# Product's groups: the bias added by GpSimd, the norm's factors held in PSUM

## The chip, the cores and the metric

The kernel runs on one core of a Trainium2 chip. The metric is device time in microseconds (us), from the launch's start to its end; lower is better. A profile is one execution of the program, with the start and end of every instruction on each engine: PE is TensorE (PEld its weight loads), DVE is VectorE, ACT is ScalarE, POOL is GpSimd, SP is SyncE, which here only issues DMAs.

## The reference

The input x is one image of 512 x 512 positions with 64 channels, in float32. Two layers are added to it in turn. The first is, cut to what matters:

```python
x = x + L0(gn(x))                       # gn: a group norm over the image

def L0(x):
    xn = ln(x, norm_w, norm_b)          # layer norm over the 64 channels
    left, right = xn @ left_w + left_b, xn @ right_w + right_b
    left, right = left * mask, right * mask         # mask[i, j] = m[i] * m[j]
    left = left * sigmoid(xn @ lgate_w + lgate_b)
    right = right * sigmoid(xn @ rgate_w + rgate_b)
    out_gate = sigmoid(xn @ ogate_w + ogate_b)
    out = einsum('bkjd,bkid->bijd', left, right)    # the triangle product
    out = ln(out, onorm_w, onorm_b) @ out_w + out_b
    return out * out_gate
```

The second layer adds a spectral convolution (the lowest 12 x 12 modes) of gn(x), computed here by small matrix products. The mask m is drawn from 0 and 1, so about half of the rows and columns of the product are zero, and there the layer norm's output is the bias alone.

## The kernel before, in words

The kernel gathers the rows with a mask that isn't zero into K = 256 slots (function compact). After two earlier stages, the triangle product of the 256 slots lies in SBUF as one tile, places, of 128 partitions x 32768 floats; a slot column has two rows of 64 channels per partition.

The stage that the change touches is one loop, from line 1075, over steps s. It is software-pipelined by hand: LEAD = 13 steps lie between the transpose of a piece (step s + 13) and its scaling (step s). The order of the instructions on each engine is the order of the code (tc.manual_schedule); no scheduler moves them. SIZE = 8 steps make a group k. The first 8 groups (first = K * 2 // 64 = 8, so 64 steps) are the **product's groups**: they take the layer norm of the triangle product, multiply it by out_w, add the bias out, and write the result u to a DRAM buffer, u_d. The 32 groups after them (256 steps) are the **x groups**: they do the layer norm and the gate of the input, multiply the gate with u (or with the bias row where the slot is masked), add it to x, take statistics and store.

A step of the product's groups, in the order of the code:

- transpose(s + 13), L927: four PE transposes into t_ps (L933), and a ScalarE copy to xt_y (L936).
- centered(s + 12), L946: sixteen PE instructions into y_ps (L954), which give for each half the centred values and the product with out_w side by side. From step 51 on, the transposes, and from step 52 on the centring, are those of x: L938 and L943 take the place of L936 and L954.
- root(k + 1) at n = 5 of the group's eight steps, L980: ScalarE takes the square root of the variances in totals and writes rss (L982).
- squared(s + 12), L962: ScalarE squares the centred half into sq_c (L971) and copies the other half to xt_c (L972). Tile xt_c has LEAD + 2 = 15 buffers.
- load(k, r), L984: gathers of x by GpSimd for the x groups, an indirect DMA of 1 MB each (L628), two for each group, three groups ahead, at n = 3 and n = 6. The first six are issued in the code at steps 43, 46, 51, 54, 59 and 62.
- summed(s + 11) at every second step, L974: VectorE reduces 128 x 1024 squares to sixteen sums in totals (L976).
- at n = 7 VectorE takes the reciprocal of rss (L1138): these are the norm's factors of the next group.
- VectorE scales the raw product with the factors, broadcast over 64 channels, into a half of z_t (L1144, 128 x 512). At every second step it adds the bias to the whole of z_t (L1147, 128 x 1024), and SP sends it to u_d (L1150, 512 KB). Tile z_t has four buffers.

At step 64, load_u(0) (L990) issues on SP the first 32 of the reads of u_d that the x groups need; each reads one slot.

In the x groups GpSimd does two operations a pair of steps, gated (L1002, a multiply) and added (L1006), both 128 x 1024.

PSUM tile scratch (L913) is one bank, [128, 4, 128] floats. Its first two rows' left halves hold totals, by the group's parity; row 2 holds the two biases, broadcast over the partitions (bias_ps), and row 3 sums for the statistics. The right halves of the first two rows are not used. The bias rows lie in SBUF as well (rows_of). GpSimd reads and writes SBUF only in this kernel.

Of the kernel before, what the change touches and what calls it, by code (L numbers as in the profile page):

```python
# [17 lines left out]
P = 128  # L18
N = 512
C = 64  # L20
# [26 lines left out]
def conv_preact_kernel(ctx: ExitStack, tc: tile.TileContext, t: dict):  # L47
    nc = tc.nc
    x, out = t["x"], t["out"]
# [562 lines left out]
    def compact(fc):  # L612
# [31 lines left out]
        with tc.tile_pool(name="xc", bufs=1) as cp:  # L644
# [48 lines left out]
            with tc.tile_pool(name="fb", bufs=QB + 8) as gp, tc.tile_pool(name="fw", bufs=2) as wk, tc.tile_pool(  # L693
# [7 lines left out]
                gts, totals, rss, rbs, xns, todo = {}, {}, {}, {}, {}, []  # L701
# [86 lines left out]
        rows_of = {}  # L788
# [17 lines left out]
        with tc.tile_pool(name="tri", bufs=1) as trp:  # L806
# [50 lines left out]
            SIZE = 8  # L857
            LEAD = 13
            RING = 5
            first = K * 2 // 64  # L860
# [3 lines left out]
            with tc.manual_schedule(), tc.tile_pool(name="late", bufs=1) as lp:  # L864
# [30 lines left out]
                with tc.tile_pool(name="np_x", bufs=LEAD + 2) as tp, tc.tile_pool(  # L895
# [17 lines left out]
                    scratch = ps_n.tile([P, 4, P], F32, name="scratch")  # L913
                    sum_ps = [scratch[:, 3, i * G : (i + 1) * G] for i in range(2)]
                    bias_ps = {"out": scratch[:, 2, :C], "ogate": scratch[:, 2, C:]}
                    for name, ps in bias_ps.items():
                        nc.vector.tensor_copy(ps, rows_of[name])
                    totals = [scratch[:, i, : SIZE * 8] for i in range(2)]
                    eps = lp.tile([P, 1], F32, name="eps")
                    nc.vector.memset(eps, EPS)  # L920
                    xts, rss, sqs, us, zs, fs, st = {}, {}, {}, {}, {}, {}, {}
# [153 lines left out]
                    for s in range(-LEAD, total_g + 2 * SIZE):  # L1075
                        k, n = divmod(s, SIZE)
# [20 lines left out]
                        if n % 2 == 0:  # L1097
                            i, c = (0, n // 2 - 1) if n >= 2 else (1, 3)
# [11 lines left out]
                        if n % 2 == 1:  # L1110
                            i, c = (0, (n - 3) // 2) if n >= 3 else (1, 3)
# [4 lines left out]
                        else:  # L1116
                            i, c = (0, (n - 4) // 2) if n >= 4 else (1, 2 + n // 2)
# [17 lines left out]
                        if 0 <= s + LEAD - 2 < total_g and (s + LEAD - 2) % 2 == 1:  # L1135
                            summed(s + LEAD - 2)
                        if n == 7 and k + 1 in rss:
                            nc.vector.reciprocal(rss[k + 1], rss[k + 1])  # L1138
                        if wps is not None:
                            c, odd = divmod(n, 2)  # L1140
                            if not odd:
                                z = zp.tile([P, 16, C], F32, name="z_t")
                            rs = rss[k][:, 8 * n : 8 * n + 8].unsqueeze(2).to_broadcast([P, 8, C])
                            nc.vector.tensor_mul(z[:, 8 * odd : 8 * odd + 8, :], wps, rs)  # L1144
                            if odd:
                                bias = bias_ps["out" if k < first else "ogate"]
                                nc.vector.tensor_add(z, z, bias.unsqueeze(1).to_broadcast([P, 16, C]))  # L1147
                                if k < first:
                                    j = JC * k + 8 * c
                                    nc.sync.dma_start(  # L1150
                                        u_d[:, j : j + 8].rearrange("p j r c -> p (j r c)"), z.rearrange("p n c -> p (n c)")
                                    )
                                else:
                                    zs[v, c] = z
# [151 lines left out]
    with tc.If(rows_with_mask < K + 1) as few:  # L1306
        with tc.tile_pool(name="fconst", bufs=1) as fc:
            compact(fc)
# [65 lines left out]
```

## Time and profile before

| what | us |
|---|---|
| median of three runs (lowest, highest) | 1879.58 (1876.83, 1881.99) |
| the profiled execution's own time | 1877.87 |
| span of its instructions | 1876.0 |
| first scaling of a product's group | 690.5 |
| first scaling of an x group | 815.5 |
| last of GpSimd's adds in the x groups begins | 1532.5 |

Over the whole span the engines are busy as follows:

| engine | busy us | share |
|---|---|---|
| PE | 1653.0 | 88% |
| PEld | 1302.6 | 69% |
| DVE | 1454.2 | 78% |
| ACT | 953.8 | 51% |
| POOL | 873.8 | 47% |

How to read it: the page cuts the span into 40 slices of 46.9 us, and gives each engine a digit a slice, its busy share in tenths. A line of a group gives the source line, engine, operation, what it writes and reads, the shapes and the count, then the busy time in us with the mean of one instruction in ns, then the idle time of the engine just before such instructions and what ended most of it. A line of waits reads "who <- for whom: us in total, how often, the longest". The bounds of a stretch (A:B) are us from the span's start, and the first number behind it is its length.

After the x groups, from about 1535 us on, a last stage reads x back, adds the second layer and writes the output; there DMA is busy at nine tenths or more and the other engines mostly wait.

### The profile page before, as it was taken

Reading aid. Unit: us, or ns where it says so; the run is one execution under the profiler, and the core shown is the slowest. Engines: PE = TensorE matmul, PEld = TensorE weight load, DVE = VectorE, ACT = ScalarE, POOL = GpSimd, SP = SyncE. Lnnn points to the kernel's source line nnn. Section 1 sums busy time; section 2 is a strip of 40 time slices with the busy share of each in tenths; the row PEclk is TensorE's granted clock in tenths of the full one; section 3 lists DMA queues with packets and bytes.
Section 4 is the critical chain, followed back from the end, with each engine's and each line's share of the span. In section 5 each row is a group of like instructions: output and inputs, shape, how many; then the busy total and the mean of one; then the engine's idle time right before and its main releaser. Section 6 shows DMA issues by size and latency. Waiting matters only on the chain. (4 is left out here: it accounts for less than half of the span.)

```text
span 1876.0 us, 33850 instructions
## 1 busy us (share of the span) xinstructions
PE 1653.0 (88%) x11598; PEld 1302.6 (69%) x11598; DVE 1454.2 (78%) x3001; ACT 953.8 (51%) x1670; POOL 873.8 (47%) x678
## 2 busy tenths in 40 slices
PE   6779899999899999899998999899989957997873
PEld 5666666664787777788887988788879835664441
DVE  5989677777455559989998899899989994664552
ACT  3665466554222278777776677677757720111000
POOL 3655111111000000059999799989979982111110
PEclk9989899999899999999999999999989976555555
DMA  6999155556655534347876677767666599999999
GB/s 251 390 380 377 59 135 139 140 138 160 206 180 175 168 127 180 136 151 263 267 258 231 226 252 252 266 222 241 235 240 229 189 252 365 414 426 427 426 427 382
DMA packets 188869, 468.23 MB, mean 250 GB/s; under 512 B 35184, under 2 KB 134384, under 8 KB 147600
## 3 DMA queue, kind: packets, MB, share of 16 engines
q1 hardware_dynamic: 158192, 262.40, 41.3%
q0 software_dynamic: 27856, 202.19, 28.0%
q8 instruction: 94, 1.54, 0.3%
q10 hardware_dynamic: 2640, 1.38, 0.3%
q14 instruction: 87, 0.71, 0.1%
HBM read 278.13 MB, written 187.76 MB: 248 GB/s over the span
## 5 line engine op out<-in xcount | busy, mean ns | idle before, releaser
L943 PE MATMUL w_ps<-gate_x,xt_c 128*128 128x128 f32 x2048 | 283.3, 283 | 30.2 <-DVE z_t L1144 28.8
L1006 POOL TENSOR_TENSOR places<-places,z_t 128x1024 f32<-128x1024 f32 x127 | 301.8, 2377 | 8.2
L943 PEld LDWEIGHTS w_ps<-gate_x,xt_c 128*128 128x128 f32 x2048 | 254.4, 195 | 47.5 <-DVE z_t L1144 45.7
L943 PE MATMUL c_ps<-center_x,xt_c 128*128 128x128 f32 x2048 | 277.7, 279 | 6.1 <-ACT xt_c L938 5.5
L943 PEld LDWEIGHTS c_ps<-center_x,xt_c 128*128 128x128 f32 x2048 | 253.5, 195 | 9.9 <-ACT xt_c L938 7.8
L1286 PE MATMUL l_ps<-places,rinv 24*128 24x512 f32 x512 | 211.3, 1128 | 33.2 <-DVE places L1293 27.1
L1051 DVE BATCH_NORM_STATS2 stats2c<-places 128x6 f32<-128x128 f32 x1024 | 220.4, 278 | 8.2 <-POOL places L1006 8.2
L976 DVE TENSOR_REDUCE scratch<-sq_c 128x16 f32<-128x1024 f32 x160 | 194.6, 1216 | 21.7 <-ACT sq_c L971 7.6
L1100 ACT ACTIVATE z_t<-z_t 128x1024 f32<-128x1024 f32 x128 | 135.4, 1058 | 141.9 <-DVE z_t L1147 120.2
L1147 DVE TENSOR_TENSOR z_t<-z_t,scratch 128x1024 f32<-128x1024 f32 x160 | 195.4, 1221 | 11.3 <-ACT rs_n L982 3.3
L1286 PEld LDWEIGHTS l_ps<-places,rinv 24*128 24x128 f32 x512 | 120.9, 304 | 118.5 <-DVE places L1293 74.8
L933 PE MATMUL t_ps<-c_ident,places 128*128 128x128 f32 x1280 | 201.4, 281 | 1.3 <-DVE places L853 1.3
L1002 POOL TENSOR_TENSOR z_t<-z_t,bias_row_out 128x1024 f32<-128x1024 f32 x63 | 149.7, 2376 | 101.2 <-ACT z_t L1100 101.0
L1293 DVE TENSOR_TENSOR places<-places,l_ps 128x512 f32<-128x512 f32 x200 | 124.0, 682 | 89.8 <-DMA places<-x_h,dst_i 58.3
L938 ACT ACTIVATE xt_c<-t_ps,ab_xc 128x512 f32<-128x512 f32 x256 | 176.1, 688 | 34.4 <-PE t_ps L933 27.7
L933 PEld LDWEIGHTS t_ps<-c_ident,places 128*128 128x128 f32 x1280 | 146.6, 143 | 59.6 <-issue 50.4
L628 POOL DMA_INDIRECT places<-in_x,src_i x64 | 62.6, 978 | 258.0 <-PE t_ps L933 247.3
L1144 DVE TENSOR_TENSOR z_t<-w_ps,rs_n 128x512 f32<-128x512 f32 x256 | 171.9, 672 | 7.4 <-PE w_ps L943 7.4
L1002 POOL TENSOR_TENSOR z_t<-z_t,places 128x1024 f32<-128x1024 f32 x64 | 151.5, 2367 | 35.9 <-ACT z_t L1100 35.7
L968 ACT ACTIVATE sq_c<-c_ps 128x512 f32<-128x512 f32 x256 | 150.7, 589 | 31.4 <-PE c_ps L943 31.1
L678 DVE BATCH_NORM_STATS2 stats1c<-x_ps 128x6 f32<-128x512 f32 x256 | 155.3, 680 | 13.4 <-PE x_ps L677 13.4
L663 ACT COPY xc<-xg 128x128 f32 x352 | 105.0, 298 | 67.5 <-POOL xc L663 43.5
(206 smaller groups left out, 2607.5 us busy)
## 6 DMA issues: line engine op xcount, KB each, us to landing
x_h<-places SPq DMA_DIRECT2D x64, 1024.0 KB
out_x<-places SPq DMA_DIRECT2D x50, 1024.0 KB
places<-u_d SPq DMA_DIRECT2D x512, 64.0 KB
left_d<-o_c SPq DMA_DIRECT2D x64, 256.0 KB
right_d<-o_c SPq DMA_DIRECT2D x64, 256.0 KB
left_raw<-left_d SPq DMA_DIRECT2D x64, 256.0 KB
right_raw<-right_d SPq DMA_DIRECT2D x64, 256.0 KB
u_d<-z_t SPq DMA_DIRECT2D x32, 512.0 KB
```

The costliest lines, as they stand in the source:

```text
L678: nc.vector.bn_stats(stats[:, 0, 16 * (jc % quarter) + 4 * r + c, :], ps.rearrange("p i k -> p (i k)"))
L933: nc.tensor.transpose(tps[:, i, :], flat[:, o : o + P], ident)
L938: nc.scalar.activation(xts[s], tps, AF.Identity, bias=ab1[:, 2:3])
L943: nc.tensor.matmul(ps[:, 2 * i : 2 * i + 2, :], xts[s][:, i, :], w, start=True, stop=True)
L968: nc.scalar.activation(sq, cps, AF.Square)
L976: nc.vector.tensor_reduce(totals[k % 2][:, 8 * (n - 1) : 8 * (n + 1)], sqs.pop(s // 2), AX.X, ALU.add)
L1002: nc.gpsimd.tensor_mul(zs[k, c], zs[k, c], u)
L1006: nc.gpsimd.tensor_add(xr, xr, zs.pop((k, c)))
L1051: nc.vector.bn_stats(st[k // 4][:, g, k % 4, :], x_of(k)[:, :, 2 * g : 2 * g + 2])
L1144: nc.vector.tensor_mul(z[:, 8 * odd : 8 * odd + 8, :], wps, rs)
L1147: nc.vector.tensor_add(z, z, bias.unsqueeze(1).to_broadcast([P, 16, C]))
L1286: nc.tensor.matmul(ps.rearrange("p j o -> p (j o)"), rinv[h, b, :], it[h], start=True, stop=True, tile_position=(32 * g, 0),)
```

## The change

It concerns the product's groups alone. Two lists of PSUM columns, factors, take the unused right halves of the first two rows of scratch. The reciprocal of a product group writes there instead of over rss in SBUF, by the group's parity, and the scaling reads its factors from there; its other operand, xt_c, and its output, z_t, stay in SBUF. The bias is added to z_t by GpSimd from the SBUF bias row, where VectorE added it from PSUM. The x groups keep factors in SBUF and the bias on VectorE. Number and size of all instructions stay the same.

```diff
                     totals = [scratch[:, i, : SIZE * 8] for i in range(2)]
+
+                    factors = [scratch[:, i, SIZE * 8 :] for i in range(2)]
...
                         if n == 7 and k + 1 in rss:
-                            nc.vector.reciprocal(rss[k + 1], rss[k + 1])
+                            nc.vector.reciprocal(factors[(k + 1) % 2] if k + 1 < first else rss[k + 1], rss[k + 1])
                         if wps is not None:
                             c, odd = divmod(n, 2)
                             if not odd:
                                 z = zp.tile([P, 16, C], F32, name="z_t")
-                            rs = rss[k][:, 8 * n : 8 * n + 8].unsqueeze(2).to_broadcast([P, 8, C])
+                            rs = (factors[k % 2] if k < first else rss[k])[:, 8 * n : 8 * n + 8]
+                            rs = rs.unsqueeze(2).to_broadcast([P, 8, C])
                             nc.vector.tensor_mul(z[:, 8 * odd : 8 * odd + 8, :], wps, rs)
                             if odd:
-                                bias = bias_ps["out" if k < first else "ogate"]
-                                nc.vector.tensor_add(z, z, bias.unsqueeze(1).to_broadcast([P, 16, C]))
+                                if k < first:
+                                    bias = rows_of["out"].unsqueeze(1).to_broadcast([P, 16, C])
+                                    nc.gpsimd.tensor_add(z, z, bias)
+                                else:
+                                    nc.vector.tensor_add(z, z, bias_ps["ogate"].unsqueeze(1).to_broadcast([P, 16, C]))
```

## The prediction

> **What bounds the kernel now.** I read the page first (its engine shares, slices and costliest groups), then the stretch of the product's groups alone. In the slices GpSimd's row shows zeros over seven of the forty slices while VectorE's climbs to 9:
>
> ```profile
> DVE  5989677777455559989998899899989994664552
> POOL 3655111111000000059999799989979982111110
> ```
>
> The end of the empty run is the product stage. The timeline puts its first scaling at 690.51 us and the first scaling of an x group (step 64) at 815.52: 64 steps in 125.0 us. Busy time over its two parts (before and after the first x transpose comes in, columns PE, PEld, DVE, ACT, POOL, each with its count) says who is full:
>
> ```profile
> 690.50:784.40 93.90, 86.97 (x1000) 71.64 (x998) 89.83 (x104) 78.57 (x156) 2.81 (x3) 0.96 0.42 166
> 784.40:815.50 31.10, 24.60 (x210) 22.41 (x208) 29.86 (x35) 19.70 (x37) 0.00 (x0) 1.00 0.33 136
> ```
>
> VectorE is busy 119.7 of 125.0 us (96%), GpSimd 2.8. PE's 87 of 93.9 looks nearly as full, but its ends are modelled, so I ask the waits of the same two parts who waited for whom:
>
> ```profile
> ACT rs_n L982 <- DVE scratch L976: 8.6, 5, 2.2
> PEld y_ps L954 <- ACT xt_y L936: 8.5, 7, 2.3
> PE y_ps L954 <- ACT xt_y L936: 6.9, 5, 2.1
> ...
> PEld c_ps L943 <- ACT xt_c L938: 6.9, 6, 1.5
> ACT xt_c L938 <- DVE z_t L1144: 5.8, 4, 1.7
> ```
>
> In the first part ScalarE's root stands still for VectorE's reduce once a group, and PE then stands still for ScalarE. In the second, ScalarE waits for a buffer of xt_c that VectorE's scaling frees. VectorE is the bound of both. Its groups in the stretch:
>
> ```profile
> L1144 DVE TENSOR_TENSOR z_t<-xt_c,rs_n 128x512 f32<-128x512 f32 x64 | 41.2, 675 | 0.0
> L976 DVE TENSOR_REDUCE scratch<-sq_c 128x16 f32<-128x1024 f32 x33 | 40.5, 1228 | 4.9 <-ACT sq_c L971 1.3 <-ACT xt_y L936 0.5
> L1147 DVE TENSOR_TENSOR z_t<-z_t,scratch 128x1024 f32<-128x1024 f32 x32 | 39.1, 1221 | 1.7
> L1138 DVE RECIPROCAL rs_n<-rs_n 128x64 f32<-128x64 f32 x8 | 4.4, 546 | 0.0
> ```
>
> The third line is what leaves VectorE. From start to start a pair of steps takes 1.14 (reduce) + 1.32 (two scalings) + 1.32 (add) = 3.78 us; 32 pairs and 8 reciprocals at 0.5 make 125.0, the measured stretch.
>
> **What the Trainium skill says.** "SBUF — State Buffer", section "Who interferes with whom": VectorE and GpSimd share a port pair; a VectorE instruction with two SBUF inputs contends with a GpSimd instruction that reads SBUF, one with at most one SBUF input does not. The trace agrees on the second half: in the x groups VectorE (busy 672 of 719.5 us, all reads of one SBUF operand at most in its large groups) runs beside GpSimd's adds, and these keep 2352 to 2399 ns. No run here shows the first half. "PSUM — Partial Sum Buffer", section "PSUM bank collisions raise a hardware error": PSUM is to be guarded by bank, not by address. The trace shows that guard: VectorE's add into z_t, which reads only the bias out of scratch, waited 3.3 us in all, 7 times, for ScalarE's root, which reads other columns of it. So the scalings will wait for the root too once they read scratch. "GPSIMD Engine Reference", section 3.1, has a two-input add of 2048 elements at 4497 ns, an estimate of some 2250 for 1024; here 2377 was measured for 1024, and I use that.
>
> **The change part by part.**
>
> *Add off VectorE.* 32 times 1.32 us, all on the path: VectorE's pair falls to 1.14 + 1.32 = 2.46, that is 1.23 a step, 1.30 with the reciprocal.
>
> *Add on GpSimd.* Nearest row: GpSimd's gating multiply of the same shapes with the same broadcast bias row, 2376 ns; its plain add takes 2377. I take 2.38 us a pair. Upper bound: if every VectorE instruction shut it out, 2.38 + 2.46 = 4.84. Below 2.35 nothing in the trace goes.
>
> *Factors into PSUM.* The scaling becomes SBUF times PSUM: rows of that kind are 682 ns (L1293, 128x512) and 1221 per 1024, against 675 now; the reciprocal keeps its input, and the two copies of it into PSUM at the stage's start (228 ns for 64 columns) show nothing dear in writing there. Between -0.05 and +0.05 us a pair; I take nothing, and VectorE's new slack (below) would hide it.
>
> *New waits.* Root and scaling now exclude each other. Per group the root waits for one more scaling (0.68 us) and the next scaling for the root (0.31). What stands behind the root on ScalarE is the square and copies that PE's next step needs. ScalarE's shortest step in the trace is 1.43 us (catching up at 685.8 to 690.3) against PE's 1.68, so 2 us a group are there to swallow it; I allow 0.2 us for each of six roots (0 to 0.6).
>
> *GpSimd's queue.* Its six gathers of the first x groups (L628) ran free before, from 671.8 to 721.3 us; now each stands behind adds and issues at loop steps 43, 46, 51, 54, 59 and 62, with a first use eight or nine steps later. SP's store of z_t now waits for GpSimd; on SP only later stores and load_u(0) stand behind it. The ring of four z_t lasts four pairs, 13.4 us at PE's pace, against 1.3 (scalings) + 2.4 (add) + 3.9 (store: issued at 814.28, load_u released at 818.16), with 1.0 for a gather ahead: 8.6. It holds.
>
> **What is late next.** *First 51 steps:* PE. While VectorE had only reduces (669.78 to 676.49) centred blocks started every 1.68 us without a wait for another engine, ScalarE in step. VectorE needs 1.30, GpSimd 1.19. So 51 x 1.68 = 85.7, plus 1.2 for roots.
> *Steps 51 to 64:* PE's step is 1.33 (789.65 to 790.98), VectorE's 1.30 plus a root wait, GpSimd's 6.5 adds x 2.38 + 4 gathers x 1.0 = 19.5 us, or 1.50 a step. GpSimd is the latest; 19.5.
> *Hand-over:* from PE's step 64 to its scaling 2.0 us (transposes, matmuls, 0.4 of waits).
> PE's step 0 was at 690.2. New first x scaling: 690.2 + 85.7 + 1.2 + 19.5 + 2.0 = 798.6, against 815.5: 16.9 us earlier.
> *Load_u(0)* starts 2.6 us after that scaling now. Then: last product scaling at -1.25, add +2.4, store +3.9 = 5.0, or 6 behind a gather. Its second half is needed 27.3 us after GpSimd's first gating (846.50 - 819.23), with a margin of some 1.8 us; 2.4 to 3.4 late less that is about 1.0 of stall.
> The x groups start with GpSimd full (19.4 of each 20 us) and VectorE full later; nothing in them is tied to an absolute time, so the rest of the program moves with their start. Sum: 16.9 - 1.0 = 15.9 earlier. The profiled execution took 1877.9 us (span 1876.0), so 1862.0; it lies 1.7 below the median of 1879.6, on which I get 1863.7.
>
> **The rivals.**
> *A, late gathers.* For: each issues only eight steps ahead now, 12 to 13 us, less GpSimd's lag of some 2. A gather moves 1 MB: at the highest rate of the slices (427 GB/s) 2.5 us plus the 2.7 that the 512 KB store shows beyond its own 1.2, so 5; in the crowded last stage 16.4 is shown (chain of waits). I take 7, hidden. At 16.4 the first is 5 late, the next pair 6, the last 3: 14 of the gain is gone, some 1877. At 11 to 13 it costs 4 to 8: 1868 to 1872. Against: the stage moves 136 to 166 GB/s now, and would move some 11 MB (six gathers, ten stores) in its last 30 us, 370 GB/s, and only there.
> *B, GpSimd and VectorE exclude each other after all, slower.* A pair would take 4.84 us against 3.78: 32 x 1.06 = 34 us later, 1914. It decides from an add of 3.8 us, 60% over the row. Against: L1006 at 2377 ns beside a VectorE 93% busy with the same kinds.
> *C, the x groups give it back.* If load_u or a buffer holds the first x groups, the start is early and the rest isn't: 1874 to 1879. Against: GpSimd ran without a gap from 819 to 862, so what holds that stage is work and not arrival.
> *D, better.* PE at 1.33 to the end, no root or load_u cost: 13 x 0.17 + 1.2 + 1.0 = 4.4 more, 1859.
>
> **How the numbers follow.** Forecast (1860 to 1868) 0.66, A up to 1874 0.14, B 0.07, C and A's worst 0.08, D below 1860 0.05. A difference of 0.3% (5.6 us) is what a measurement of this kernel can tell from no change. Faster, below 1874: forecast, A, D = 0.85; within: 0.08; slower: 0.07. The range 1858.5 to 1871 takes the forecast, nearly all of D and half of A: 0.78.
>
> **What would show it.** Right: the first x scaling at 797 to 801 us; between 690 and 780 root waits of no more than 0.6 us, PE's centred blocks every 1.68; VectorE 70 to 80% busy there; GpSimd's adds 2.35 to 2.40. Wrong: adds above 3 us (B); PE's transposes of steps 51, 55, 59 idle for a DMA (A); GpSimd idle around its sixth gating multiply by more than 2 us, or an x stage longer than 719.5 us (C).

## The result and the profile after

The changed kernel takes 1861.23 us (median of seven runs, 1853.9 to 1870.46), the kernel before 1877.41 (seven runs, 1875.18 to 1882.31): a ratio of 0.9911, 95% interval 0.9886 to 0.9937, or 16.2 us less. Predicted were 1863.7. The profiled execution of the changed kernel took 1864.07 (span 1862.3).

In the slices, VectorE's and GpSimd's rows now rise together: GpSimd's zeros end two slices earlier, and VectorE's nines of the product stage become eights.

```profile
DVE  5989677777455548888997999899979984665452
POOL 3656111111000006888998899899979981212110
```

The product's groups run from the first scaling at 691.7 us to the first x scaling at 797.75. Their two parts, split at 777 us, just behind the first x transposes (775.1; columns PE, PEld, DVE, ACT, POOL with counts, clock, DMA share, GB/s):

```profile
691.70:777.00 85.30, 85.30 (x1020) 70.63 (x1019) 68.48 (x83) 80.29 (x160) 61.84 (x28) 1.00 0.44 173
777.00:797.75 20.75, 19.60 (x171) 18.87 (x170) 17.46 (x21) 16.48 (x30) 18.21 (x11) 1.00 0.87 322
```

They last 106.05 us, not 125.0. VectorE went from 96% to 81% busy; in the first part it is at 80% and PE at 100%. PE's centred blocks (L956) start every 1.68 us, one behind the other:

```profile
718.64 1.16 PE L956 MATMUL y_ps<-both,xt_y 64*128 64x128 f32 x16
719.73 0.66 PE L935 MATMUL t_ps<-c_ident,places 128*128 128x128 f32 x4
720.32 1.16 PE L956 MATMUL y_ps<-both,xt_y 64*128 64x128 f32 x16
```

Among the waits of the stretch from 690 to 785 us, PE now waits for another engine for 0.6 us only, once. It is VectorE that waits, for ScalarE's squares and for the root. The largest waits are:

```profile
POOL z_t L1151 <- DVE z_t L1147: 242.1, 20, 222.4
DVE scratch L978 <- ACT sq_c L973: 8.8, 14, 1.1
PEld y_ps L956 <- issue: 8.7, 52, 0.2
DVE z_t L1147 <- ACT rs_n L984: 6.3, 7, 1.2
```

(222.4 us of the first line is GpSimd's idle time ahead of the stage.) VectorE's groups and GpSimd's add in the stage:

```profile
L1147 DVE TENSOR_TENSOR z_t<-xt_c,scratch 128x512 f32<-128x512 f32 x64 | 42.5, 685 | 9.6 <-ACT rs_n L984 6.7
L978 DVE TENSOR_REDUCE scratch<-sq_c 128x16 f32<-128x1024 f32 x32 | 39.3, 1228 | 10.3 <-ACT sq_c L973 7.7 <-DVE z_t L1147 0.8
...
L1151 POOL TENSOR_TENSOR z_t<-z_t,bias_row_out 128x1024 f32<-128x1024 f32 x32 | 75.9, 2370 | 246.2 <-DVE z_t L1147 242.1 <-issue 3.0 <-POOL z_t L1151 0.9
```

The add took 1221 ns on VectorE and takes 2370 on GpSimd, and the stage is shorter: GpSimd's time lies beside PE's. From the same two profiled executions, stage by stage:

| us from the span's start | before | after | earlier by |
|---|---|---|---|
| first product scaling | 690.5 | 691.65 | -1.1 |
| first x scaling | 815.5 | 797.75 | 17.8 |
| GpSimd's first x instruction | 819.2 | 803.05 | 16.2 |
| GpSimd's ninth x add | 867.8 | 853.7 | 14.1 |
| GpSimd's last x add | 1532.5 | 1519.9 | 12.6 |
| end of the span | 1876.0 | 1862.3 | 13.7 |

The stage gains 19 us; it began 1.1 us later in this execution, so the first x scaling comes 17.8 earlier, and 4 of these are given back by the end. The experiments ask two things: which part of the change makes the gain and what bounds the stage now, and where the part that was given back went.

### The profile page after: what moved, and what is told of

Its sections match the earlier page's. It is cut to its first block, busy times and chain, and to the rows that moved or that the text cites. A ratio compares the mean times of both kernels' runs of the same rounds, so it can differ in the third digit from the quotient of the medians.

```text
span 1862.3 us, 33900 instructions
## 1 busy us (share of the span) xinstructions
PE 1650.4 (89%) x11598; PEld 1300.6 (70%) x11598; DVE 1421.6 (76%) x2969; ACT 953.2 (51%) x1670; POOL 949.5 (51%) x710
## 5 line engine op out<-in xcount | busy, mean ns | idle before, releaser
L1151 POOL TENSOR_TENSOR z_t<-z_t,bias_row_out 128x1024 f32<-128x1024 f32 x32 | 75.9, 2370 | 246.2 <-DVE z_t L1147 242.1
L678 DVE BATCH_NORM_STATS2 stats1c<-x_ps 128x6 f32<-128x512 f32 x256 | 155.5, 680 | 13.7 <-PE x_ps L677 12.7
L1153 DVE TENSOR_TENSOR z_t<-z_t,scratch 128x1024 f32<-128x1024 f32 x128 | 156.3, 1221 | 9.9 <-ACT rs_n L984 3.7
L1004 POOL TENSOR_TENSOR z_t<-z_t,bias_row_out 128x1024 f32<-128x1024 f32 x63 | 149.6, 2374 | 7.9 <-ACT z_t L1102 7.7
L732 POOL COPY rbc<-rq_out 128x512 f32<-128x512 f32 x64 | 38.3, 613 | 214.0 <-DVE rq_out L209 155.1
```

The source lines that it names most:

```text
L678: nc.vector.bn_stats(stats[:, 0, 16 * (jc % quarter) + 4 * r + c, :], ps.rearrange("p i k -> p (i k)"))
L1004: nc.gpsimd.tensor_mul(zs[k, c], zs[k, c], u)
L1153: nc.vector.tensor_add(z, z, bias_ps["ogate"].unsqueeze(1).to_broadcast([P, 16, C]))
```

## The experiments

My theory: VectorE's 3.78 us a pair were the bound, and PE's 3.36 took their place; the place of the factors matters because it keeps scaling and add from excluding each other; what is given back goes through SP's reads of u_d. The main rivals: the place of the factors is worth nothing, or is the gain itself; GpSimd or ScalarE is the new bound; the x groups have their own pace.

**Factors in SBUF, bias on GpSimd.**

```diff
-nc.vector.reciprocal(factors[(k + 1) % 2] if k + 1 < first else rss[k + 1], rss[k + 1])
+nc.vector.reciprocal(rss[k + 1], rss[k + 1])
...
-rs = (factors[k % 2] if k < first else rss[k])[:, 8 * n : 8 * n + 8]
+rs = rss[k][:, 8 * n : 8 * n + 8]
```

> The bias is added by GpSimd as in the change, but the factors stay in SBUF, so VectorE's scaling reads two operands from SBUF. If such a scaling and a GpSimd instruction that reads SBUF exclude each other, as the Trainium skill states, a pair of steps needs at least 2.37 (add) + 1.28 (two scalings) = 3.65 us, with the reduce beside the add: the 64 steps from the first scaling to the first of an x group take 117 to 125 us (125.0 before, 106.1 with the change), GpSimd's add or VectorE's scaling reads longer than 2.37 us or 0.68 us, and the whole takes 1870 to 1878. Rival: they don't disturb each other, and the factors' place is worth nothing: 104 to 107 us for the 64 steps, 2.37 and 0.68 us each, about 1861.

Measured: 118.9 us for the 64 steps (691.8 to 810.7), 1873.18 in the whole, ratio to before 0.9973 (0.9963 to 0.9983). VectorE's and GpSimd's timelines of this kernel (start, length, engine, line):

```profile
719.12 1.21 DVE L978 TENSOR_REDUCE scratch<-sq_c 128x16 f32<-128x1024 f32 x1
720.24 2.60 DVE L1147 TENSOR_TENSOR z_t<-xt_c,rs_n 128x512 f32<-128x512 f32 x2
722.77 1.21 DVE L978 TENSOR_REDUCE scratch<-sq_c 128x16 f32<-128x1024 f32 x1
723.90 2.60 DVE L1147 TENSOR_TENSOR z_t<-xt_c,rs_n 128x512 f32<-128x512 f32 x2
```

```profile
719.33 2.37 POOL L1151 TENSOR_TENSOR z_t<-z_t,bias_row_out 128x1024 f32<-128x1024 f32 x1 [1.69 <-DVE z_t L1147]
722.98 2.36 POOL L1151 TENSOR_TENSOR z_t<-z_t,bias_row_out 128x1024 f32<-128x1024 f32 x1 [1.29 <-DVE z_t L1147]
```

The add runs from 719.33 to 721.70. VectorE's reduce goes on beside it; its two scalings start at 720.24 and together read 2.60 us, not 1.28: the first stands until the add is done. The next add begins at 722.98, 0.14 us after these scalings; it adds to what they write, so it has to wait for them in any case. The period is 3.65 us, the sum of the two. So with the factors in SBUF the move to GpSimd is worth 6 us of the stage; both halves of the change together are worth 19. The rival, that the factors' place is worth nothing, falls.

**Factors in PSUM, bias on VectorE.**

```diff
-if k < first:
-    bias = rows_of["out"].unsqueeze(1).to_broadcast([P, 16, C])
-    nc.gpsimd.tensor_add(z, z, bias)
-else:
-    nc.vector.tensor_add(z, z, bias_ps["ogate"].unsqueeze(1).to_broadcast([P, 16, C]))
+bias = bias_ps["out" if k < first else "ogate"]
+nc.vector.tensor_add(z, z, bias.unsqueeze(1).to_broadcast([P, 16, C]))
```

> The factors lie in PSUM as in the change, but VectorE still adds the bias. If the gain is the add that leaves VectorE, the 64 steps stay at VectorE's 3.78 us a pair, and the new wait between root and scaling adds 0 to 0.8 us a group: 125 to 131 us, the whole 1877 to 1884. Rival: reading one operand from PSUM makes the scaling itself faster, and part of the gain is there: scalings under 0.65 us, and fewer than 123 us.

Measured: 134.4 us for the 64 steps (690.9 to 825.3), 1888.31 in the whole, ratio 1.0046 (1.0032 to 1.0060). The direction is as expected; the stage is 3 us and the whole 4 us over what was expected. VectorE's timeline of the kernel before, then of this one:

```profile
740.25 1.23 DVE L976 TENSOR_REDUCE scratch<-sq_c 128x16 f32<-128x1024 f32 x1
741.39 1.28 DVE L1144 TENSOR_TENSOR z_t<-xt_c,rs_n 128x512 f32<-128x512 f32 x2
742.71 1.22 DVE L1147 TENSOR_TENSOR z_t<-z_t,scratch 128x1024 f32<-128x1024 f32 x1
744.03 1.23 DVE L976 TENSOR_REDUCE scratch<-sq_c 128x16 f32<-128x1024 f32 x1
```

```profile
723.59 1.23 DVE L978 TENSOR_REDUCE scratch<-sq_c 128x16 f32<-128x1024 f32 x1
724.86 1.29 DVE L1147 TENSOR_TENSOR z_t<-xt_c,scratch 128x512 f32<-128x512 f32 x2
726.18 1.22 DVE L1150 TENSOR_TENSOR z_t<-z_t,scratch 128x1024 f32<-128x1024 f32 x1
727.50 1.23 DVE L978 TENSOR_REDUCE scratch<-sq_c 128x16 f32<-128x1024 f32 x1
```

From reduce to scaling it is 1.27 us where it was 1.14, the pair takes 3.91 where it took 3.78, and 32 x 0.13 = 4 of the 9.4 us are that. Another 3.1 us are eight waits of VectorE's scalings for ScalarE's root, which in turn had stood for a scaling (13.1 us in six waits between 690 and 800); the last 2 us are not accounted for. Alone, this half costs 9 us of the stage and the other half gains 6; together they gain 19, so the two can't be added up.

**PE's transposes issued twice.**

```diff
-for i in range(4):
-    o = (8 * n + 2 * i) * C
-    nc.tensor.transpose(tps[:, i, :], flat[:, o : o + P], ident)
+for i in range(8 if k < first else 4):
+    o = (8 * n + 2 * (i % 4)) * C
+    nc.tensor.transpose(tps[:, i % 4, :], flat[:, o : o + P], ident)
```

> The change with each of the four PE transposes of a product step issued twice, into the same place; the result is the same. Four transposes take PE 0.59 us from start to start. If PE bounds the first 51 steps now, each step grows from 1.68 to 2.27 us: the 64 steps from 106.1 to 135 to 138 us, and the whole by 36 to 40 us (the 13 steps ahead of the first scaling grow too), to 1896 to 1902. Rival: ScalarE (1.43 a step at its fastest) or VectorE (1.30) with their waits are the real bound and PE's busy time is only modelled: the step grows by less than 0.3 us, and the whole by less than 20.

Measured: 128.5 us for the 64 steps (691.8 to 820.3), 1884.72 in the single run. PE's timeline:

```profile
722.54 1.16 PE L956 MATMUL y_ps<-both,xt_y 64*128 64x128 f32 x16
723.63 1.09 PE L935 MATMUL t_ps<-c_ident,places 128*128 128x128 f32 x8
724.66 1.16 PE L956 MATMUL y_ps<-both,xt_y 64*128 64x128 f32 x16
```

Expected were 135 to 138 us and 1896 to 1902, so both numbers missed. A step takes 2.12 us (722.54 to 724.66), where it took 1.68: four more transposes cost 0.44 and not 0.59, which had included the change over to the centred block. 51 x 0.44 = 22.4 us, and the stage grew by 22.4. What was added to PE appears in the stage in full, so PE is the bound of the first 51 steps; I had mis-sized what I added.

**The add twice on GpSimd.**

```diff
 nc.gpsimd.tensor_add(z, z, bias)
+nc.gpsimd.tensor_mul(z, z, rows_one.unsqueeze(1).to_broadcast([P, 16, C]))
```

> The change with a second GpSimd instruction of the same size behind each add (a multiply of z_t with ones). A pair of steps then takes GpSimd 4.75 us, more than PE's 3.36 and more than the 3.78 of the kernel before, so GpSimd becomes the bound, and the price from which GpSimd's part turns the change into a loss can be read: the 64 steps take 32 x 4.75 + 4 gathers, 152 to 158 us, and the whole 1906 to 1916. Rival: the instructions overlap on GpSimd, or PE's wait is longer than shown: under 140 us.

Measured: 148.1 us for the 64 steps (691.6 to 839.7) and 1911.2 in the single run. GpSimd is busy 143.5 of the 148.1, its instructions lie back to back at 4.76 us a pair, and its last one begins at 850.3, 10.5 us after the first x scaling: the ring of z_t lets VectorE run ahead. So the stage, read at VectorE, is shorter than the 152 to 158 us that I wrote, and the whole is in the range. Who waits now:

```profile
DVE z_t L1149 <- DMA u_d<-z_t: 48.2, 24, 3.4
PE t_ps L937 <- DMA places<-in_x,src_i: 13.1, 4, 4.3
```

VectorE stands for a buffer of z_t until the store behind GpSimd has gone out. It shows the other side of the change: at 4.76 us a pair, over PE's 3.36, GpSimd sets the stage; where between the two it begins was not tried. And PE stands for gathers that are late because they queue on GpSimd. That is the prediction's rival A, which appears here and not in the change.

**No add at all.**

```diff
-nc.gpsimd.tensor_add(z, z, bias)
+pass
```

> The change without the addition of the bias in the product's groups: u lacks the bias where it isn't masked, all else is as in the change. If PE sets these groups and GpSimd's adds are off the path, the first 51 steps stay at 1.68 us and the 64 steps at 105 to 106.5 us (106.1 with the change); only the store of the last piece goes out 2.4 us earlier, and with it the reads of u_d: 1 to 3.5 us less in the whole. Rival: GpSimd's adds still hold the loop through the ring of z_t: 100 to 103 us for the 64 steps and 4 us or more less in the whole.

This kernel leaves the bias out of u. Measured: 105.8 us for the 64 steps (690.2 to 796.0), against 106.1 with the add; 1852.69, ratio 0.9887 (0.9867 to 0.9906). The add is hidden in the stage to within 0.3 us. By the ratios the whole is 4.5 us less than with the change, where 1 to 3.5 were expected, but the intervals overlap. GpSimd, with nothing to do, also issued its gathers early (671 to 719 us), and the last store went out sooner; GpSimd's ninth add of the x groups comes 42.95 us after its first, against 47.1 with the change. The next three runs take that apart.

**Six gathers three groups earlier.**

```diff
-if 0 <= v + 3 < len(units):
+ahead = v + 6 if v < -3 else v + 3
+if 0 <= ahead < len(units) and (ahead < 3) == (v < -3):
     if n == 3:
-        load(v + 3, 0)
+        load(ahead, 0)
```

> The change, with the six gathers of the first three x groups issued three groups earlier (at steps 19 to 38, not 43 to 62). If GpSimd is the latest engine of the last 13 steps, because four gathers stand among its adds there, these steps fall from 20.75 us to 18 to 19 (PE's own 1.33 a step is 17.3), the first 51 stay at PE's 1.68 us a step, and the first scaling of an x group comes 1.5 to 3 us earlier; the whole is 1 to 3 us less than the change. Rival: VectorE, with its waits for the root, sets these steps: 20 to 21 us as before.

Measured: 106.1 us for the 64 steps (690.7 to 796.8), no change; 1859.09, ratio 0.9903 (0.9880 to 0.9925), not to be told from the change. My reading that GpSimd is the latest engine of the last 13 steps is wrong. But SP's first read of u_d now starts 3.8 us after the last store of u_d is issued (798.12 to 801.96), and 5.3 in the changed kernel (799.42 to 804.69), where the last gather, at 796.04, had lain just ahead of that store. GpSimd's ninth add comes 46.1 us after its first, 1.0 sooner than with the change.

**The second batch of reads behind the first stores.**

```diff
-if n == 4 and v % 2 == 0 and 0 <= v < len(units) - 2:
+if n == 4 and v % 2 == 0 and 0 < v < len(units) - 2:
     load_u(v // 2 + 1)
+if n == 4 and v == 1:
+    load_u(1)
```

> The change, with the second batch of 32 reads of u_d (load_u(1)) issued a group later, behind the first stores of x. If the 2.1 us that the changed kernel gave back between GpSimd's fourth and eighth add of the x groups come from the SP queue (64 reads of u_d, 43 us, ahead of the first store, for which GpSimd's gather into the same place waits), the gather's wait of 4.5 us there is gone, GpSimd's ninth add comes 4 to 5 us earlier against its first, and the whole takes 2 to 4.5 us less than the change. Rival: the gather waits for the store's transfer or for its data's last reader and not for its place in the queue: the wait stays within 1 us of 4.5.

What this is aimed at, in the changed kernel: SP's timeline, then GpSimd's, at the start of the x groups.

```profile
799.42 0.33 SPq L1156 DMA_DIRECT2D u_d<-z_t  x1
804.69 43.11 SPq L995 DMA_DIRECT2D places<-u_d  x64
847.92 3.06 SPq L1024 DMA_DIRECT2D x_h<-places  x4
```

```profile
845.81 2.37 POOL L1004 TENSOR_TENSOR z_t<-z_t,bias_row_out 128x1024 f32<-128x1024 f32 x1
852.69 0.98 POOL L628 DMA_INDIRECT places<-in_x,src_i  x1 [4.51 <-PE c_ps L945]
```

The gather at 852.69 writes the place that the first store reads, and that store is issued at 847.92, behind 64 reads. Before, the store was issued at 861.99 and the gather ran at 866.76 after 2.4 us of idling: both 14.07 us later, while GpSimd's own work was 16.2 later. The engine that the trace names as releaser, PE, is not the cause: the gather moves with the store.

Measured with the edit: the gather doesn't wait, so its place behind the 64 reads was the cause. But GpSimd waits elsewhere, and its ninth add comes 46.9 us after its first, against 47.1; 1860.20, ratio 0.9898 (0.9876 to 0.9920), not to be told from the change. Its timeline:

```profile
833.44 2.36 POOL L1004 TENSOR_TENSOR z_t<-z_t,places 128x1024 f32<-128x1024 f32 x1 [4.17 <-PE t_ps L935]
...
851.44 0.98 POOL L628 DMA_INDIRECT places<-in_x,src_i  x1
```

In this execution the first read started only 7.9 us after the last store was issued (798.35 to 806.26; here too a gather, at 794.97, lay just ahead), and the multiply at 833.44 is the first that needs the second half of the batch. The prediction had named this wait, the experiment had not. In the changed kernel the same multiply, at 830.28, did not wait: there the first read came 1.6 us after GpSimd's first x instruction, here 4.3. The edit touches nothing ahead of that read, so its lateness is not the edit's, and what the edit alone gains when the read is in time stays open.

**Both.** The last two edits together:

```diff
+ahead = v + 6 if v < -3 else v + 3
...
+if n == 4 and v == 1:
+    load_u(1)
```

> The change with both edits: the first six gathers three groups earlier, and the second batch of reads of u_d behind the first stores of x. The theory after the two single runs: the hand-over to the x groups is set by when SP's first read of u_d starts and by what stands behind the reads on SP. With the late reads alone the gather's wait was gone, but the first batch, itself late behind a store of u_d that shared the DMA engines with a gather, held GpSimd's sixth gating multiply for 4.2 us instead. With no gather beside the last stores the first read starts 3.9 us after the last of them, so neither wait is left: GpSimd's ninth add of the x groups comes 42.5 to 43.5 us after its first (47.1 with the change, 46.1 and 46.9 with the single edits), and the whole is 4 to 6 us below the change. Rival: something else holds GpSimd there (the x groups' own pace): 46 to 47 us again, and no difference to the change.

Measured: 106.1 us for the 64 steps (687.8 to 793.9); SP's first read 3.8 us after the last store; neither wait is left, and GpSimd's ninth add comes 42.8 us after its first:

```profile
842.04 2.36 POOL L1004 TENSOR_TENSOR z_t<-z_t,bias_row_out 128x1024 f32<-128x1024 f32 x1
...
844.57 0.98 POOL L628 DMA_INDIRECT places<-in_x,src_i  x1 [0.16 <-issue]
845.57 2.37 POOL L1008 TENSOR_TENSOR places<-places,z_t 128x1024 f32<-128x1024 f32 x1
```

In the kernel before it came 45.0 us after, with 2.4 us of the same wait. So the change gave back 2.1 us here, and the two edits take away these and 2.2 more.

The whole takes 1850.79 us, ratio 0.9870 (0.9849 to 0.9891), the lowest of all. By the ratios it is 8 us below the change's 0.9911, with intervals that just overlap. Of these, 4.3 are seen at the ninth add (47.1 to 42.8), but they do not last in the execution that was profiled, which at 1859.49 us was the longest of its five: from the ninth add to the last it took 670.1 us, the changed kernel 666.2. So it is shown that the two waits go; that the whole gains by it is likely and not shown.

## Why the prediction was right, point by point

**VectorE as the bound, its add as the gain.** Right. With the add left on it, the stage isn't shorter (134.4 us).

**The add on GpSimd.** 2.38 us expected, 2.370 measured, beside a VectorE that reads one operand from SBUF. Rival B was not idle: with two operands it is what happens, for the scalings alone (3.65 us a pair; I had 4.84, with every VectorE instruction shut out).

**Factors in PSUM.** Wrong in size: I took nothing, with 0.05 us a pair as the bound; it is 0.13 from reduce to scaling. In the changed kernel the way from a pair's last scaling to the next reduce is longer too, 0.79 us against 0.60 with factors in SBUF. VectorE's slack hides both, as the text said.

**Where the sum starts.** Misread by one step. The 690.2 us that I took for PE's step 0 is the start of step 1; step 0 began at 688.5. With the right start the same terms give 796.9 and not 798.6.

**The first 51 steps.** PE's transposes of steps 0 and 51 start at 689.53 and 775.10: 85.57 us, against 85.7, and the 1.2 for the roots did not come. VectorE waits for the root instead of ScalarE for VectorE: 6.3 us in seven waits, the longest 1.2, where I had named no more than 0.6 as a sign. They fall into VectorE's slack.

**Steps 51 to 64.** The number is right by luck: 19.5 us expected, 19.7 measured (775.10 to 794.78). I had GpSimd set it, and PE did: its short step of 1.33 us makes 17.3 of it, and four longer ones, in part waits for ScalarE (0.59 and 0.41 us), the rest. GpSimd was busy for 18.2 of the last 20.75 us, but its adds began within 1 us of the end of their scalings, and moving its gathers away left the 13 steps at 19.7 (774.18 to 793.87).

**The hand-over.** From PE's step 64 to the first x scaling 2.0 us were expected, 2.97 measured. From PE's step 0 to there I had 108.4, and it was 108.2; this execution's step 0 was 1.0 later than before's. So 797.75 met the 798.6 because the roots' 1.2 too much, the hand-over's 1.0 too little, the step misread and the late start cancel. From there to GpSimd's first x instruction it is 5.3 us, and 3.7 before. ScalarE's table load of 1.28 us for the sigmoid lay in a wait for VectorE before; now it stands behind two squares that wait for PE (0.98 and 0.99 us) and is on the path. I hadn't seen that.

**The reads of u_d.** 1.0 expected, 2.1 measured (16.2 to 14.1), and by another way. The first read starts 6.9 us after the first x scaling, where 5 to 6 were expected. The text looked for the wait at the multiply that needs the second half; it was at a gather, behind a store, behind 64 reads on SP. What failed is the sentence on what stands behind SP's store of z_t: "only later stores and load_u(0)" left out what stands behind load_u in turn.

**The rest of the way.** "Nothing in them is tied to an absolute time" holds: between the ninth and the last add the gain went from 14.1 to 12.6 us, in small steps at the fetches of the modes, which VectorE waits for three times (20.7 us in all after, 18.8 before). In other runs these steps go both ways (664.7 us from the ninth to the last add before, 666.2 with the change, 660.7 with early gathers, 670.1 with both edits), so I don't put them down to the change; what sets them, and the 16 us spread of the changed kernel's runs, stays open.

**The rivals.** A (late gathers) did not occur: PE waits for no DMA in the stage. C did in part: its sign, longer x groups, came true. From the first x scaling to GpSimd's last add it is 722.1 us, and 716.9 before.

**The total.** 15.9 us were expected and 16.2 measured between the medians; the two profiled executions differ by 13.8. That the medians agree so closely is luck in part: 16.9 at the first x scaling were 17.8, 1.0 given back were 4.1 by the end of the profiled span, and the changed kernel's seven runs spread over 16 us. The mechanism, an add off VectorE and PE as the next bound, is what the experiments bear out.

## What to carry to other kernels

An elementwise step that doubles in length on GpSimd can still shorten a stage that VectorE bounds, if its new time fits under the next engine's, here 2.37 us a pair under PE's 3.36. What stays on VectorE beside it should not read two operands from SBUF: here moving one operand to PSUM cost 9 us alone and was worth 13 beside the move. When a stage gets shorter, follow each DMA queue from its last instruction in the stage to the first engine that waits behind it, through every instruction in between.

## What the runs showed of the hardware that I had not expected

A VectorE scaling with both inputs in SBUF stands until a GpSimd add that is under way is done; a reduce with one SBUF input (1.21 us) runs through, and with one input in PSUM the scalings and the adds keep their times (685 and 2370 ns). "SBUF — State Buffer", section "Who interferes with whom", in the Trainium skill says that the two contend in the first case and not in the others. That an add also stands for such a scaling is not shown: in these kernels each add waits for its own data at that point.

From a reduce into a PSUM tile to a scaling that reads its factors from the same tile takes 1.27 us, where it took 1.14 with factors in SBUF. An operand in PSUM as such is not the cause. In the x groups the scaling reads another PSUM tile, w_ps, and starts 1.12 us after the reduce (kernel before):

```profile
854.87 1.21 DVE L976 TENSOR_REDUCE scratch<-sq_c 128x16 f32<-128x1024 f32 x1
855.99 0.68 DVE L1144 TENSOR_TENSOR z_t<-w_ps,rs_n 128x512 f32<-128x512 f32 x1
```

There, and with factors in SBUF, the scaling starts 0.09 us before the reduce's record ends, with factors in the reduce's own tile 0.03 us after it. So the price is that of reading the tile that the instruction before writes; factors in a PSUM tile of their own were not tried.

A 512 KB store released the read behind it after 3.8 to 3.9 us in seven of the ten kernels. It took 5.3, 7.2 and 7.9 us in the three where a 1 MB gather had been issued 3.4 us ahead of it (the change, transposes twice, second batch later). With the gather 3.95 us ahead, in the kernel with factors in SBUF, it took 3.9 again. What makes 5.3 or 7.9 of the same 3.4 us stays open.
